# First tile's softmax weights: turned in 32 by 32 blocks by VectorE and put in place by transfers, with the table of the feed-forward blocks laid out anew

## The chip, the cores and the metric

The kernel runs on one core of one Trainium2 chip. The metric is the device time in microseconds (us) of one execution. Five queues matter: PE (TensorE, with PEld for its weight loads), DVE (VectorE), ACT (ScalarE), POOL (GpSimd) and SP (SyncE, which issues transfers and does no arithmetic). Each works through its instructions in the order in which the program issues them; between queues only semaphores wait.

## The reference

Sixteen sequences of 256 tokens with 128 features go through four residual blocks, each applied to a layer-normed copy: a state-space block, a feed-forward block, a power-attention block, and the feed-forward block again.

```python
x = x + ssm(layernorm(x))
x = x + ffn(layernorm(x))
x = x + power_attention(layernorm(x))
x = x + ffn(layernorm(x))
```

The change touches only the feed-forward blocks. Each has two layers, and a layer holds windowed attention and then a gated hidden stage:

```python
qkv = shift_token(x) @ wqkv                # 8 heads of 64
q, k = rotary(l2norm(q) * qs, l2norm(k) * ks)
sim = where(mask, -inf, q @ k.T * 8)       # windows of 64: own window and the one before, 128 keys
x = x + (softmax(sim) @ v) @ wo
h = layernorm(shift_token(x)) * lg + lb
a, g = split(h @ w1 + b1)
x = x + (a * gelu(g)) @ w2 + b2
```

With 256 tokens a sequence has four windows. The kernel takes the first 128 tokens as tile 0 (keys 0 to 127 for all of its queries) and the last 128 as tile 1 (each half of its queries with another 128 keys).

## The kernel before

**Stages.** The program runs the state-space block, feed-forward block 1, the power block and feed-forward block 3, with a little overlap between neighbours. A feed-forward block (`ffn_block`, line 737) handles 32 items, 16 sequences times two layers, in 16 groups of two (n = 2g and 2g + 1).

**The table.** Lines 1111 to 1127 hold one period as a list of words, written out by hand or by a program, in the order of issue. In `we0.1:4` the letters are the step (`stages`, line 1102), the digits its part (tile, half, chunk), `.1` says which of the two sequences of the group, and `:4` how many periods that group lags behind. So one pass through the table works on several groups at different stages. Every engine is wrapped in `Pinned` (line 79), which keeps the written order on each queue, SP among them. Within each engine a step that has to wait holds up all that stands behind it. No step is moved at run time.

**Softmax weights.** For each sequence and tile: `mask` (k, ACT writes the band into a pair of PSUM banks), `scores` (s, PE adds q k), `maxima` (mx, DVE), `less_maximum` (lm, DVE, into SBUF tile `pr`, queries on partitions), `exponentials` (e, ACT), `sums` (su, DVE with a reciprocal), `weights_of` (wo, POOL multiplies). To multiply by the values PE needs keys on partitions: `turn_weights` (wt, line 972) turns one half of the heads, four 128x128 transposes into a PSUM bank, and `turned_weights` (wc, line 980) copies the bank to `prT` on ACT. Then `weigh` (we, line 985, PE), `weighed` (oc, ACT), `mix` (mi, PE) and `mixed` (ma, DVE adds to `u_all`). There is one pair of banks for scores, and six single banks for everything else.

**What SP carries.** `values_out` (vc, line 883) ends for tile 1 with two transfers that make the half-shifted keys' values. `mixed` (ma, line 1013) ends for tile 1 with three transfers that write the shifted tokens into `shifted`; `unit_stats` (Us, line 1029) reads them, tile by tile, with four `bn_stats` of which the last two need the transfers of the group's second sequence. After Us come `unit_factors` (Uf) and `unit_norm` (Un) on POOL, `unit_turn` (Ut) on PE and the gated hidden stage (Ur, Ug, Um, Ud, Ua).

**Memory.** All feed-forward tiles are cut from one SBUF tile, `mem`, by an `Arena` (line 570): an early region from the bottom up and a late one (`FFN_LATE`, lines 732 to 735) up to the top. On the page and in the trace all of them are called `mem`, and nearly every instruction is put down to line 88, the line of `Pinned` that records it.

Of the kernel before, what the change touches and what calls it, by code (L numbers as in the profile page):

```python
# [12 lines left out]
F32 = mybir.dt.float32  # L13
# [7 lines left out]
P = 128  # L21
# [10 lines left out]
WINDOW = 64  # L32
# [13 lines left out]
def kernel(ctx: ExitStack, tc: tile.TileContext, io, out: bass.AP):  # L46
# [555 lines left out]
    class Banks:  # L602
# [11 lines left out]
        def bank(self, q, key, shape, name):  # L614
            b = next((b for b in self.free if b not in self.kept), self.free[0])
            self.free.remove(b)
            self.taken[id(q), key] = b
            q[key] = shaped(self.singles[b][: shape[0], : int(np.prod(shape[1:]))], shape)
            return q[key]

        def give_back(self, q, key):
            self.free.append(self.taken.pop((id(q), key)))
            return q.pop(key)
# [27 lines left out]
    NP = HEADS // 2  # L651
# [77 lines left out]
            layers.append(dict(wq=wq, wo=wo, w1=w1, w2=w2, b1=b1, b2=b2, lg=lg, lb=lb, rope=rope))  # L729
        fw.update(bands=bands, primer=primer, layers=layers)  # L730

    FFN_LATE = [("rn", 32, 2), ("qkT", 2048, 2), ("vx", 1536, 4), ("pr", 1024, 3), ("prT", 1024, 2), ("oT", 512, 2)]
    FFN_LATE += [("mx", 8, 4), ("rl", 8, 4), ("shifted0", 512, 1), ("shifted1", 512, 1), ("hn", 512, 1)]
    FFN_LATE += [("hnT", 512, 1), ("hid", 1536, 1), ("ub", 512, 1)]
    FFN_LATE += [(f"ln_{x}4", 4 * n, 4) for x, n in (("st", 6), ("mv", 2), ("r", 1), ("mr", 1))]

    def ffn_block(k, fw, store, shared):


        mem, ps, pe, dve, act, pool, sp = shared  # L740
        bank, give_back = ps.bank, ps.give_back
        sb = Arena(
            mem,
            [("hT0", 256, 1), ("hT1", 256, 1), ("sq", 512, 2), ("m2", 1024, 2), ("m", 512, 8), ("ss", 32, 2)]
            + [(f"ln_{x}2", 2 * n, 4) for x, n in (("st", 6), ("mv", 2), ("r", 1), ("mr", 1))],
            FFN_LATE, mem.shape[1] - sum(n * c for _, n, c in FFN_LATE),
        )
# [8 lines left out]

        hTs = [sb.tile([P, L], F32, f"f{k}_hT{i}", f"hT{i}") for i in range(2)]
        shifted = [sb.tile([P, GT, D], F32, f"f{k}_shifted{i}", f"shifted{i}") for i in range(2)]
        first = []

        def begin():
# [154 lines left out]
        def mask(n, q, t):  # L916

            psim = q["sim", t] = ps.pair(q, ("sim", t)).rearrange("p r (h k) -> p r h k", h=NP)


            if not first:
                first.append(n)
                for r in range(2):
                    pe.matmul(psim[:, r].rearrange("p h k -> p (h k)"), identb, fw["primer"], start=True, stop=True)
                for h in shifted:
                    pool.memset(h[:1, 0::2, HD:], 0.0)
            act.copy(
                psim.rearrange("p r h k -> p (r h) k"), fw["bands"][t].unsqueeze(1).to_broadcast([P, 2 * NP, P])
            )
# [47 lines left out]
            sb.free(pr, 2)  # L977


        def turned_weights(n, q, t, r):  # L980
            if r == 0:
                q["prT", t] = sb.tile([P, 2, NP, P], F32, name=f"f{k}_prT_{n}_{t}", tag="prT")
            act.copy(q["prT", t][:, r], give_back(q, ("ppt", t, r)))

        def weigh(n, q, t):

            prT, vx = q.pop(("prT", t)), q["vx"]
            po = bank(q, ("po", t), [P, NP, P], f"f{k}_po_{n}_{t}")
            for p in range(NP):
                for w in range(t + 1):  # L990
                    qs = slice(w * WINDOW, (w + 1) * WINDOW) if t else slice(0, P)
                    for r in range(2):
                        pe.matmul(
                            po[r * DH : (r + 1) * DH, p, qs], vx[:, 2 - w if t else 0, 2 * p + r, :],
                            prT[:, r, p, qs], start=True, stop=True,
                        )
            sb.free(prT)
            sb.free(vx, 2)


# [91 lines left out]
        def unit_sum(g, q):  # L1092
# [10 lines left out]
            ns=norm_stats, nf=norm_factors, n=norm, ut=turn_tokens, uc=turned_tokens, p=project, sq=squares,  # L1103
            ro=rotate, ss=square_sums, ra=rotated, v=values, vc=values_out, b=bounded, i=inverses,
            nw=newton, no=normed, t=turn, tc=turned, k=mask, s=scores, mx=maxima, lm=less_maximum,
            e=exponentials, su=sums, wo=weights_of, wt=turn_weights, wc=turned_weights, we=weigh,
            oc=weighed, mi=mix, ma=mixed, Us=unit_stats, Uf=unit_factors, Un=unit_norm, Ut=unit_turn,
            Uc=unit_turned, Ur=unit_rise, Ug=unit_gate, Um=unit_gated, Ub=unit_base, Ud=unit_fall,
            Ua=unit_sum,
        )  # L1110
        period = """
            ns.0:0 Uf:5 p00.0:2 e1.1:4 ma0.0:4 ro01.0:2 t11.0:3 s0.0:3 tc11.0:3 ro11.1:3 oc1.0:4
            v0.0:2 sq00.0:2 su1.1:4 ra11.1:3 Ud0:6 vc0.0:2 Un:5 mx0.0:3 t10.0:3 wt00.1:4 ss00.0:2
            tc10.0:3 wt01.1:4 lm0.0:3 wc00.1:4 Ud1:6 ra01.0:2 wc01.1:4 i.1:3 mi1.0:4 n.0:1 wo1.1:4
            p11.0:2 ma1.0:4 Ua:6 v1.0:2 ro00.0:2 nw.1:3 sq11.0:2 k1.0:3 p10.0:2 ss01.0:2 ra00.0:2
            vc1.0:2 p00.1:2 ro11.0:2 Ut:5 no00.1:3 s1.0:3 Uc:5 no01.1:3 e0.0:3 we0.1:4 mx1.0:3
            ra11.0:2 sq10.0:2 nf.1:1 oc0.1:4 ut.0:1 wt10.1:4 ss10.0:2 wt11.1:4 lm1.0:3 wc10.1:4
            Ur10:5 uc.0:1 wc11.1:4 Ur11:5 ss11.0:2 e1.0:3 ro10.0:2 b.0:2 we1.1:4 no11.1:3 k0.1:3
            su0.0:3 ra10.0:2 t00.1:3 oc1.1:4 v0.1:2 tc00.1:3 su1.0:3 no10.1:3 t01.1:3 vc0.1:2
            p01.1:2 sq00.1:2 wo0.0:3 Ur12:5 tc01.1:3 ss00.1:2 sq01.1:2 ro00.1:2 mi0.1:4 i.0:2 Ug:5  # L1120
            wo1.0:3 s0.1:3 ma0.1:4 ro01.1:2 mi1.1:4 nw.0:2 Ur01:5 ma1.1:4 mx0.1:3 ra00.1:2 p10.1:2
            ss01.1:2 t10.1:3 Ub:5 sq10.1:2 Um1:5 t11.1:3 tc10.1:3 v1.1:2 lm0.1:3 tc11.1:3 no00.0:2
            wt00.0:3 vc1.1:2 wt01.0:3 no01.0:2 ss10.1:2 ns.1:0 wc00.0:3 p01.0:1 ro10.1:2 wc01.0:3
            no11.0:2 Ur00:5 k1.1:3 ra01.1:2 wt11.0:3 Um0:5 e0.1:3 wt10.0:3 Us:4 we0.0:3 n.1:1
            ra10.1:2 wc10.0:3 sq01.0:1 s1.1:3 oc0.0:3 su0.1:3 wc11.0:3 ut.1:1 p11.1:2 mx1.1:3
            wo0.1:3 Ur02:5 uc.1:1 Um2:5 t00.0:2 t01.0:2 no10.0:2 tc00.0:2 lm1.1:3 we1.0:3 sq11.1:2
            tc01.0:2 nf.0:0 mi0.0:3 ss11.1:2 k0.0:2 b.1:2
        """
        parts = []
        for word in period.split():  # L1130
# [3 lines left out]
        for i in range(N // GS + max(lag for *_, lag in parts)):  # L1134
            for j, (step, part, which, lag) in enumerate(parts):
                g = i - lag
                if 0 <= g < N // GS:
                    n = g if which is None else g * GS + int(which)
# [362 lines left out]
    for block, length, ahead in (  # L1501
        (ffn_block(1, fw, False, shared), 39.2, 0.0), (power_block(w, dram, shared), 20.5, 60.0),
        (ffn_block(3, fw, True, shared), 39.2, 20.0),
    ):
        begin, work = block
        start = end - ahead
        line.append((start, begin, ()))
        line += [(start + at * length, step, args) for at, step, args in work]
        end = max(at for at, *_ in line)
# [55 lines left out]
```

## Time and profile before

| what | value |
|---|---|
| median of 3 runs | 2170.4 us (2170.24 to 2171.72) |
| the profiled execution's own time | 2171.14 us |
| its span, first to last instruction | 2169.3 us |
| mean granted TensorE clock | 0.981 |
| PE, DVE, ACT, POOL busy | 94%, 85%, 79%, 88% of the span |
| feed-forward blocks, roughly | 500 to 1140 us and 1510 to 2169 us |

An instruction's record runs from its start to its end; on PE and DVE records of neighbours overlap a little, so that what one more instruction costs is the step from one start to the next. A line of the table of windows gives a stretch of the span, its length, and then for PE, PEld, DVE, ACT and POOL the busy time with the number of instructions in brackets, the granted TensorE clock, the share of the transfer engines and their GB/s. A line of a timeline gives start, length, engine, source line, operation, output and input with shapes, and how many like it follow each other; in brackets at its end stands the idle time before it and who ended it. SPq is SP's own queue of transfer issues.

### The profile page before, as it was taken

What the parts mean: (1) busy time and instruction counts of PE and PEld (TensorE: products, weight loads), DVE (VectorE), ACT (ScalarE), POOL (GpSimd) and SP (SyncE); (2) the same over time, 40 slices, a digit from 0 to 9 for tenths busy, and PEclk for the clock granted to TensorE, in tenths of its full rate; (3) what the DMA queues carried; (4) which work ended last, traced back from release to release, by engine and by line L of the source; (5) the groups of instructions that cost most, each with busy time, mean ns of one, the idle gap of its engine ahead of it and who ended that gap; (6) DMA issues with size and microseconds to landing.
All of it is one profiled execution on the core that took longest, in us unless ns stands there. A gap on an engine that the chain in (4) does not pass through costs nothing.

```text
span 2169.3 us, 44282 instructions
## 1 busy us (share of the span) xinstructions
PE 2028.6 (94%) x16172; PEld 1331.3 (61%) x16174; DVE 1841.5 (85%) x3285; ACT 1706.5 (79%) x2879; POOL 1899.4 (88%) x2183
## 2 busy tenths in 40 slices
PE   5999999877999999999998999998899999999997
PEld 2344444334667777777765777775567777777775
DVE  2999999997989888888856999997988888888873
ACT  4777777746888887887865999997788887878874
POOL 7999999967999888888967999996999988888993
PEclk8999999998999999999997999999999999999998
DMA  4333333321001110111103323230010111101110
GB/s 93 97 83 81 98 80 79 79 52 24 18 22 23 23 23 17 23 23 23 23 11 118 101 98 119 84 114 9 21 23 17 23 23 23 23 16 33 28 28 23
DMA packets 97350, 104.21 MB, mean 48 GB/s; under 512 B 51458, under 2 KB 63596, under 8 KB 97132
## 3 DMA queue, kind: packets, MB, share of 16 engines
q1 hardware_dynamic: 96444, 101.22, 18.4%
q8 instruction: 128, 2.10, 0.4%
q14 instruction: 90, 0.74, 0.1%
q10 hardware_dynamic: 688, 0.15, 0.1%
HBM read 40.28 MB, written 2.36 MB: 20 GB/s over the span
## 4 chain that ended last, share of the span: by engine, by line
PE 54%; POOL 17%; DVE 9%; ACT 9%; issue 7%; DMA 2%; SPq 2%; POOLq 0%; DVEq 0%; ACTq 0%
PE bank L88 44%; POOL bx L88 7%; PE pair L88 7%; POOL mem L88 7%; DVE mem L88 6%; ACT mem L88 5%; DVE hs L88 2%; ACT pair L88 2%; SPq L88 2%; POOL hs L88 1%; PE xe_ps L88 1%; DMA mem<-u_all 1%; DMA bb<-reps 1%; POOL sf L88 1%; PE y_ps L88 1%
## 5 line engine op out<-in xcount | busy, mean ns | idle before, releaser
L88 POOL TENSOR_TENSOR mem<-mem 128x256 f32<-128x256 f32 (+5 forms) x1328 | 1156.7, 901 | 88.4 <-DVE mem L88 66.2
L88 ACT COPY mem<-bank 128x512 f32<-128x512 f32 (+4 forms) x1152 | 590.7, 556 | 147.6 <-PE bank L88 142.0
L88 PEld LDWEIGHTS bank<-ident,mem 128*128 128x128 f32 x3104 | 353.5, 141 | 171.2 <-issue 109.4
L88 PE MATMUL bank<-ident,mem 128*128 128x128 f32 x3104 | 426.0, 277 | 15.1 <-POOL mem L88 10.2
L88 PE MATMUL bank<-wqkv,mem 128*128 128x512 f32 x768 | 385.8, 607 | 1.8 <-ACT mem L88 1.8
L88 DVE TENSOR_REDUCE mem<-mem 128x8 f32<-128x512 f32 (+1 forms) x384 | 325.6, 849 | 9.8 <-ACT mem L88 9.4
L88 DVE TENSOR_TENSOR mem<-bank,rope 128x1024 f32<-128x1024 f32 x256 | 308.8, 1216 | 24.1 <-POOL mem L88 15.8
L88 DVE TENSOR_TENSOR_SCAN hs<-a,bx 128x1024 f32<-128x1024 f32 x128 | 291.4, 2281 | 38.6 <-POOL bx L88 35.5
L88 POOL TENSOR_TENSOR bx<-dx,bb 128x1024 f32<-128x1024 f32 x128 | 298.5, 2357 | 4.0 <-DVE hs L88 3.3
L88 ACT ACTIVATE mem<-mem 128x1024 f32<-128x1024 f32 (+2 forms) x384 | 280.2, 735 | 24.4 <-DVE mem L88 16.3
L88 PE MATMUL pair<-mem 64*64 64x128 f32 (+2 forms) x4096 | 256.7, 296 | 22.0 <-DVE mem L88 13.5
L88 PE MATMUL y_ps<-hs,ident 128*128 128x512 f32 x512 | 242.8, 599 | 11.4 <-DVE hs L88 6.7
L88 PEld LDWEIGHTS pair<-mem 64*64 64x64 f32 (+2 forms) x4096 | 194.9, 160 | 74.2 <-issue 26.2
L88 ACT ACTIVATE a<-delta,neg_a 128x510 f32<-128x510 f32 x256 | 176.0, 689 | 79.1 <-DVE hs L88 73.5
L88 ACT ACTIVATE mem<-bank 128x512 f32<-128x512 f32 (+1 forms) x272 | 160.6, 591 | 62.9 <-PE bank L88 58.6
L88 PE MATMUL bank<-mem 128*64 128x64 f32 (+2 forms) x4608 | 203.3, 255 | 5.3 <-ACT mem L88 2.9
L88 PE MATMUL bank<-mem,w 128*128 128x512 f32 x384 | 193.5, 603 | 3.8 <-ACT mem L88 3.8
L88 PEld LDWEIGHTS bank<-mem 128*64 128x64 f32 (+1 forms) x4608 | 156.8, 128 | 64.3 <-issue 30.1
L88 PEld LDWEIGHTS y_ps<-hs,ident 128*128 128x128 f32 x512 | 95.7, 190 | 154.4 <-issue 125.8
L88 DVE TENSOR_REDUCE mem<-pair 128x8 f32<-128x1024 f32 x128 | 153.2, 1197 | 30.3 <-PE pair L88 29.6
L88 PEld LDWEIGHTS bank<-wqkv,mem 128*128 128x128 f32 x768 | 128.9, 194 | 72.4 <-issue 60.2
L88 DVE TENSOR_TENSOR mem<-pair,mem 128x1024 f32<-128x1024 f32 x128 | 155.5, 1215 | 0.4
(130 smaller groups left out, 2827.0 us busy)
## 6 DMA issues: line engine op xcount, KB each, us to landing
bb<-reps SPq DMA_DIRECT2D x128, 256.0 KB
mem<-pngd SPq DMA_DIRECT2D x64, 512.0 KB
mem<-mem SPq DMA_DIRECT2D x128, 128.0 KB
mem<-u_all SPq DMA_DIRECT2D x64, 64.0 KB
mem<-u_all SPq DMA_DIRECT2D x64, 63.5 KB
x_all<-in_resid_dram SPq DMA_DIRECT2D x8, 256.0 KB
out_dram<-x_all SPq DMA_DIRECT2D x8, 256.0 KB
wqkv<-in_wqkv_dram SPq DMA_DIRECT2D x6, 256.0 KB
```

What stands on the lines that cost most here:

```text
L88: bi = getattr(self.eng, name)(*args, **kw)
```

## The change

In feed-forward blocks tile 0's weights no longer go through PE and ACT. `wt00`, `wt01`, `wc00` and `wc01` leave the table, and two steps enter it. `blocks_turned` (bt) is one DVE instruction over 128x1024 float32 numbers, which turns each 32 by 32 block in its place. `blocks_moved` (bm) issues nine transfers on SP, each of 32 partitions by 1 KB from SBUF to SBUF, one for each block of queries i and block of keys j that the windows allow (1 + 2 + 3 + 3); the rest of the target, `pry0` for even and `pry1` for odd items, is set to zero once for each block of the program, by POOL in the first `mask`. `weigh` for tile 0 reads its moving operand from there, in four runs of 32 numbers in place of one of 128. The late region grows by 4096 numbers for each partition. Tile 1 stays as it was. The table has a new order throughout, with some lags changed (among them Uf and Un from 5 to 4, p00.0 and sq00.0 from 2 to 1, p01.0 and sq01.0 from 1 to 2); its length in the plan that interleaves the blocks stays 39.2.

```diff
+    FFN_LATE = [("rn", 32, 2), ("pry0", 1024, 1), ("pry1", 1024, 1), ("prx", 1024, 2), ("qkT", 2048, 2), ...
...
+        turned_ = [sb.tile([P, NB, 2 * NP, BS], F32, f"f{k}_pry{i}", f"pry{i}") for i in range(2)]
...
+                for y in turned_:
+                    pool.memset(y, 0.0)
...
+        def blocks_turned(n, q):
+            x = q["x"] = sb.tile([P, NB, 2 * NP, BS], F32, name=f"f{k}_prx_{n}", tag="prx")
+            pr = q["pr", 0].rearrange("p r h (b k) -> p b (r h) k", k=BS)
+            dve.transpose(x, pr)
+            sb.free(q["pr", 0])
+
+        def blocks_moved(n, q):
+            x, y = q.pop("x"), turned_[n % 2]
+            q["y"] = y
+            for i in range(NB):
+                for j in range(max(0, i - WINDOW // BS), i + 1):
+                    sp.dma_start(y[j * BS : (j + 1) * BS, i], x[i * BS : (i + 1) * BS, j])
+            sb.free(x)
...
+            if t == 0:
+                prT = q.pop("y").rearrange("k b (r h) q -> k r h b q", r=2)
...
-                            prT[:, r, p, qs], start=True, stop=True,
+                            prT[:, r, p] if t == 0 else prT[:, r, p, qs], start=True, stop=True,
```

The new table, in the words that the prediction follows (the whole has 163 words in place of 167):

```
ns.0:0 we1.0:4 ro01.1:3 bm.1:4 no10.0:3 ut.1:2 ro00.0:2 s0.0:3 ... mx0.0:3 ... vc1.1:3 su1.1:4 ...
lm0.0:3 ... ma0.0:4 ss00.0:2 ... ro01.0:2 ... ma1.0:4 Ua:6 we0.1:4 ss01.0:2 ... ss10.0:2 s1.0:3 ...
su0.0:3 ... mx1.0:3 ... ro10.0:2 ... lm1.0:3 ... ss11.0:2 ... wo0.0:3 ro11.0:2 ... su1.0:3 ...
ro00.1:2 wo1.0:3 mi0.1:4 Ug:5 bt.0:3 s0.1:3 ra11.0:2 ma0.1:4 bm.0:3 mi1.1:4 mx0.1:3 p11.1:2
no11.1:3 ma1.1:4 ss00.1:2 Ur00:5 lm0.1:3 sq11.1:2 p10.1:2 n.0:1 i.0:2 ro11.1:2 nw.0:2 t10.1:3
v0.1:2 tc10.1:3 ra00.1:2 Um0:5 sq10.1:2 Ur02:5 ss11.1:2 e0.1:3 ut.0:1 no00.0:2 Um2:5 t11.1:3
ns.1:0 we0.0:3 su0.1:3 ... ro10.1:2 oc0.0:3 s1.1:3 vc1.0:2 ... Us:4 ... mx1.1:3 ... Uf:4 ...
ss10.1:2 ... Um1:5 ... lm1.1:3 ... ss01.1:2 Un:4 sq00.0:1 bt.1:3 tc01.0:2 mi0.0:3 k0.0:2
```

More of the change, by code (lines that the diff above doesn't have):

```diff
@@ L730, in ffn_weights @@
         fw.update(bands=bands, primer=primer, layers=layers)
-    FFN_LATE = [("rn", 32, 2), ("qkT", 2048, 2), ("vx", 1536, 4), ("pr", 1024, 3), ("prT", 1024, 2), ("oT", 512, 2)]
+    FFN_LATE = [("rn", 32, 2), ("pry0", 1024, 1), ("pry1", 1024, 1), ("prx", 1024, 2), ("qkT", 2048, 2), ("vx", 1536, 4), ("pr", 1024, 3), ("prT", 1024, 2), ("oT", 512, 2)]
     FFN_LATE += [("mx", 8, 4), ("rl", 8, 4), ("shifted0", 512, 1), ("shifted1", 512, 1), ("hn", 512, 1)]
@@ L758, in ffn_block @@
         shifted = [sb.tile([P, GT, D], F32, f"f{k}_shifted{i}", f"shifted{i}") for i in range(2)]
+        BS = 32
+        NB = P // BS
+        turned_ = [sb.tile([P, NB, 2 * NP, BS], F32, f"f{k}_pry{i}", f"pry{i}") for i in range(2)]
         first = []
@@ L985, in weigh @@
         def weigh(n, q, t):
-            prT, vx = q.pop(("prT", t)), q["vx"]
+            vx = q["vx"]
+            if t == 0:
+                prT = q.pop("y").rearrange("k b (r h) q -> k r h b q", r=2)
+            else:
+                prT = q.pop(("prT", t))
             po = bank(q, ("po", t), [P, NP, P], f"f{k}_po_{n}_{t}")
@@ L994, in weigh @@
                             po[r * DH : (r + 1) * DH, p, qs], vx[:, 2 - w if t else 0, 2 * p + r, :],
-                            prT[:, r, p, qs], start=True, stop=True,
+                            prT[:, r, p] if t == 0 else prT[:, r, p, qs], start=True, stop=True,
                         )
-            sb.free(prT)
+            if t == 1:
+                sb.free(prT)
             sb.free(vx, 2)
@@ L1105, in ffn_block @@
             nw=newton, no=normed, t=turn, tc=turned, k=mask, s=scores, mx=maxima, lm=less_maximum,
-            e=exponentials, su=sums, wo=weights_of, wt=turn_weights, wc=turned_weights, we=weigh,
+            e=exponentials, su=sums, wo=weights_of, wt=turn_weights, wc=turned_weights, bt=blocks_turned, bm=blocks_moved, we=weigh,
             oc=weighed, mi=mix, ma=mixed, Us=unit_stats, Uf=unit_factors, Un=unit_norm, Ut=unit_turn,
@@ L1111, in ffn_block @@
         period = """
[L1112 to L1127, printed above, removed]
+            ns.0:0 we1.0:4 ro01.1:3 bm.1:4 no10.0:3 ut.1:2 ro00.0:2 s0.0:3 b.1:3 uc.1:2 no11.0:3
@@ new lines, in ffn_block @@
+            e1.1:4 Ud0:6 mx0.0:3 ra01.1:3 i.1:3 oc1.0:4 vc1.1:3 su1.1:4 t10.0:3 nw.1:3 Ud1:6
+            tc10.0:3 lm0.0:3 wo1.1:4 p01.0:2 nf.0:1 ma0.0:4 ss00.0:2 t11.0:3 sq01.0:2 mi1.0:4
+            no00.1:3 tc11.0:3 ro01.0:2 k1.0:3 Ut:5 p10.0:2 ra00.0:2 ma1.0:4 Ua:6 we0.1:4 ss01.0:2
+            sq10.0:2 no01.1:3 e0.0:3 ss10.0:2 s1.0:3 Uc:5 ra01.0:2 su0.0:3 wt10.1:4 Ub:5 wt11.1:4
+            wc10.1:4 nf.1:1 p11.0:2 mx1.0:3 oc0.1:4 wc11.1:4 t00.1:3 ro10.0:2 Ur11:5 tc00.1:3
+            sq11.0:2 v0.0:2 lm1.0:3 ra10.0:2 t01.1:3 vc0.0:2 ss11.0:2 Ur12:5 tc01.1:3 wo0.0:3
@@ new lines, in ffn_block @@
+            ro11.0:2 e1.0:3 p00.1:2 k0.1:3 we1.1:4 su1.0:3 b.0:2 no10.1:3 sq00.1:2 Ur10:5 oc1.1:4
+            ro00.1:2 wo1.0:3 mi0.1:4 Ug:5 bt.0:3 s0.1:3 ra11.0:2 ma0.1:4 bm.0:3 mi1.1:4 mx0.1:3
+            p11.1:2 no11.1:3 ma1.1:4 ss00.1:2 Ur00:5 lm0.1:3 sq11.1:2 p10.1:2 n.0:1 i.0:2 ro11.1:2
+            nw.0:2 t10.1:3 v0.1:2 tc10.1:3 ra00.1:2 Um0:5 sq10.1:2 Ur02:5 ss11.1:2 e0.1:3 ut.0:1
+            no00.0:2 Um2:5 t11.1:3 ns.1:0 we0.0:3 su0.1:3 tc11.1:3 no01.0:2 k1.1:3 v1.0:2 ra11.1:2
+            ro10.1:2 oc0.0:3 s1.1:3 vc1.0:2 vc0.1:2 Us:4 wo0.1:3 Ur01:5 uc.0:1 n.1:1 wt10.0:3
@@ L1128, in ffn_block @@
+            mx1.1:3 wt11.0:3 Uf:4 wc10.0:3 p01.1:2 ss10.1:2 wc11.0:3 p00.0:1 Um1:5 sq01.1:2 ra10.1:2
+            lm1.1:3 t00.0:2 t01.0:2 tc00.0:2 v1.1:2 ss01.1:2 Un:4 sq00.0:1 bt.1:3 tc01.0:2 mi0.0:3
+            k0.0:2
         """
```

## The prediction

> **What bounds the kernel now.** I read the shares and slices of the page first, then engine sums by stretch, then timelines of PE, DVE and SP inside one period, and last SP's rows.
>
> ```profile
> PE 2028.6 (94%) x16172; PEld 1331.3 (61%) x16174; DVE 1841.5 (85%) x3285; ACT 1706.5 (79%) x2879; POOL 1899.4 (88%) x2183
> PE   5999999877999999999998999998899999999997
> ...
> 545.00:584.00 39.00, 36.66 (x376) 26.69 (x376) 36.46 (x62) 31.52 (x60) 37.68 (x54) 1.00 0.10 22
> 623.74:662.82 39.08, 39.08 (x357) 27.99 (x357) 35.15 (x57) 32.96 (x60) 37.14 (x56) 1.00 0.10 22
> 858.24:897.32 39.08, 39.08 (x357) 27.99 (x357) 33.59 (x49) 31.60 (x56) 33.67 (x44) 1.00 0.10 22
> ```
>
> The table of windows shows it: from 623.7 to about 1107 us (12.4 periods) PE is busy for all of each 39.08 us period, and block 3 repeats this. PE is the only bound there; DVE idles 5.5 us of a late period. In the first periods, while norm statistics (ns, nf, n) still run, DVE has 35.15 and POOL 37.14; two such periods, 623.7 to about 702, are PE-bound, and the two before them are bound by POOL (37.7 of 39.0).
>
> **PE and ACT: removed.** The timeline of PE, one period:
>
> ```profile
> 882.38 1.04 PE L88 MATMUL bank<-ident,mem 128*128 128x128 f32 x8
> 883.25 1.02 PE L88 MATMUL bank<-wqkv,mem 128*128 128x512 f32 x2
> ```
>
> Eight transposes take 0.87 us from start to start, 0.108 each; a period loses 16: 1.73 us. PE's new sum is 39.08 - 1.73 = 37.35. ACT loses four 0.59 us copies and bounds nothing. `weigh` keeps its matmuls; for its split moving operand I take the same price (nearest: 633 ns for the convolution's split 128x512 operand against 595 to 607, so 0 to 6% of 2 x 1.03 us, under 0.15 us).
>
> The Trainium skill ("VectorE: DVE Perf Modes", Rules for kernel authors) advises TensorE for a 128x128 transpose where the result may land in PSUM, and VectorE only for 32x32 blocks within a bank: a rule against this change. Its table (The three transpose paths) gives TensorE 390 ns for bf16; by that, as an estimate, the removed part would be 16 x 0.39 = 6.2 us of a period; by the row it is 1.73, and the row decides.
>
> **DVE: added.** No block transpose is in the trace. Bounds for 128x1024: 0.60 (step after a 128x512 reduce, in case two numbers go per cycle) and 2.26 us (two passes of the 1.13 step); I take 1.2, the recorded length of other 128x1024 float32 instructions (1193 to 1216 ns). DVE's sum becomes 33.59 + 2 x 1.2 = 36.0 late, 37.5 early: still at or under PE.
>
> **SP: added, and in the way.** Nine transfers for each item stand in one run. The rows of SP, and the timeline of SP and DVE round Us:
>
> ```profile
> 9.77 1.82 SPq L166 DMA_DIRECT2D wd2T<-in_wd2T_dram  x4
> 786.47 4.64 SPq L88 DMA_DIRECT2D mem<-u_all  x3
> 791.22 1.20 SPq L88 DMA_DIRECT2D mem<-mem  x2
> ...
> L88 SPq DMA_DIRECT2D mem<-mem x128: 461/549/1512, 503.7 to 2089.6; - x128
> L88 SPq DMA_DIRECT2D mem<-pngd x64: 319/320/433, 1143.2 to 1449.8; - x64
> ...
> 2084.15 4.65 SPq L88 DMA_DIRECT2D mem<-u_all  x3
> 2091.20 0.29 DVE L88 BATCH_NORM_STATS2 mem<-mem 128x6 f32<-128x128 f32 x1 [0.37 <-DMA mem<-u_all]
> ```
>
> One issue, d, costs between 0.37 (320 ns plus a 0.05 gap) and 0.65 (0.60 each in the x2 row plus a gap); I take 0.50, between the nearest in shape (wd2T, 16 rows of 1 KB, 0.455 each) and the nearest in kind (SBUF to SBUF, 0.60). A run is 9 x 0.50 = 4.5 us. SP's sum is harmless (2 x (4.65 + 1.20 + 4.5) = 20.7 of 37), its order is not: in the new table bm.0 stands directly ahead of ma1.1, so the three transfers of `mixed` queue behind it. From their first issue to the third `bn_stats` of Us (the one that reads them) is 7.05 us in the rows above.
>
> [...]
>
> **The loop.** bt.0 on DVE 1.2, bm.0 on SP 4.5, the transfers of ma1.1 7.1, then DVE in written order until bt.0 of the next period. That work, by steps from start to start in the late period: the last two statistics 0.8; mx 3 x 1.13; su 3 x 1.36; lm 3 x 1.13; ro 6 x 1.13; ss 6 x 0.60; bt.1 1.2; Um1 0.67; Ua 0.60; two ma 0.4: 24.9 us. Sum 1.2 + 4.5 + 7.1 + 24.9 = 37.7. This exceeds PE's 37.35, though DVE's own sum is 36.0: DVE stands idle for some 2 us before Us. Early, ns.0 adds 0.8: 38.5. POOL's way round (Us, Uf, Un ... wo0.0, bt.0) has about 21.4 us in place of 24.9 late, 24.2 in place of 25.7 early, and does not decide. Meshing: before, nothing is lost; in the power stage (1250 to 1450) the fullest engine, ACT, shows 49.3 to 49.6 of 50; I add 0.2. Late 37.9, early 38.7.
>
> y's own transfers are nearly hidden: 1.2 + 4.5 + 2.4 (7.05 - 4.65, from the last issue to use) = 8.1 us from bt.0; PE has s0.1, mi1.1, five 0.87 projections, two turns and ut.0, 7.5 us, before we0.0. The 0.6 left over fits in PE's slack, 37.9 - 37.35. If PE were late, weigh, v1.0 and s1.1 behind it would be late too.
>
> **Once per block.** At its end, where nothing covers it, tile 0 takes 8.1 us in place of two turns and two copies (2 x (0.43 + 0.59) = 2.0); tile 1 follows tile 0 by mask, scores, mx and lm (1.03 + 1.05 + 1.13 + 1.13 = 4.3) and hides part of that, while we0.1 stands ahead of wt10.1 on PE: 3 us (0 to 6). Two memsets of 128x1024 on POOL at 952 ns (row of the power block's), in a stretch where POOL is full: 1.0 (0 to 1.9). The larger late region now overlaps the power block's `vx`, whose zeroing stands half a period behind the last we0 in the plan: nothing.
>
> **Sum.** A block: late 10.4 x (39.08 - 37.9) = 12.3; two early x (39.08 - 38.7) = 0.8; the two before them 0, POOL's load being the same; less 3 and 1: 9.1. Two blocks 18.2. From the profiled execution's 2171.1: 2152.9; the median lies 0.7 lower: **2152 us**.
>
> **Rivals.**
> - *PE stays the bound* (d at 0.37 to 0.42; for: transfers of the power block at 320 ns; against: all SBUF-to-SBUF ones at 0.46 and more). Loop 36.5 to 37.0, period 37.35 + 0.2: 10.4 x 1.53 + 2 x 1.0 - 2.5 = 15.4, two blocks 31: 2140. With nothing lost at all, 2 x 12.4 x 1.73 = 43: 2127.
> - *Slower: SP's queue.* Same loop at d = 0.65: 39.05 + 0.2 late, 40.05 early. Block: -1.8, -1.9, the two before -1, end -4, memset -1.9: -10.6; 2192. It decides from d = 0.58, where 9.1 is used up (each 0.1 of d is 0.9 us in 12.4 periods). For: the x2 row; against: that row follows the long u_all transfers directly.
> - *Slower: block transpose at 2.26.* Both bt lie in the loop: 37.9 + 2.1 = 40.0, early 40.8; -9.6 - 3.4 - 2 - 5: -20 a block; 2210. Decides from about 1.6 us.
> - *Nothing to measure:* d near 0.56 to 0.60, gains and once-per-block costs cancel: 2166 to 2175.
>
> That the change does something else than it says is out: the built order holds 64 block transposes, 576 small transfers and 512 fewer turns.
>
> **How the numbers follow.** Under 0.2% (4.3 us) a difference can't be told from none. Forecast (d 0.43 to 0.56, 2144 to 2166) 0.35, PE stays the bound 0.25, nothing to measure 0.11, SP slower 0.20, transpose slower 0.09. Faster 0.60, same 0.11, slower 0.29. Range: 2130 (between 2140 and 2127) to 2194, which takes in SP's rival and leaves out the slow transpose.
>
> **What would show it.** Period in PE's chain: 37.4 PE-bound, 37.7 to 38 loop, 39 and over SP. DVE's third `bn_stats` of Us idle on "DMA mem<-u_all" by about 2 us each period; SP's run x9 of 4.1 to 5.9 us with u_all's x3 right behind; StreamTranspose near 1.2 us; PE idle about 0.5 us a period, on ACT's mask or on the new transfers. Wrong if DVE never waits at Us (the loop is not there), if PE waits longest at we0 (y's way is the bound), or if the new order loses a microsecond elsewhere.

## The result and the profile after

The changed kernel takes 2233.5 us (median of four runs, 2231.2 to 2237.1) beside 2171.0 us for the kernel before on the same chip: 1.029 times as long, 95% interval 1.0276 to 1.0301. The forecast was 2152 us, a gain of 18 us, with a range up to 2194; the change costs 62 us instead.

The page of the changed kernel, its shares of busy time and PE's forty slices:

```profile
PE 2004.3 (90%) x15662; PEld 1282.4 (58%) x15662; DVE 1909.2 (86%) x3349; ACT 1662.9 (75%) x2751; POOL 1903.7 (85%) x2187
...
PE   6999999867899999999978999997789999999986
```

PE is busy for 24 us less than before (2028.6 to 2004.3), and for 90% of a longer span in place of 94%: in the slices of the feed-forward blocks the nines at both ends of a block give way to eights and a seven.

Three windows of 39 us, about a period, with the columns of the windows shown before the forecast; the first is at the start of a feed-forward block, the second early in it, the third late:

```profile
556.00:595.00 39.00, 33.54 (x338) 23.06 (x336) 34.64 (x56) 27.34 (x51) 33.39 (x49) 0.96 0.15 36
638.50:677.74 39.24, 36.77 (x331) 24.87 (x330) 35.82 (x58) 31.49 (x54) 35.27 (x50) 1.00 0.15 34
863.81:903.05 39.24, 38.37 (x345) 26.21 (x348) 35.62 (x52) 30.11 (x51) 33.68 (x45) 1.00 0.15 37
```

From the first transfer of one `ma1.1` to that of the next, a late period is 39.24 us (860.33 to 899.57), against 39.08 before, although PE has sixteen turns less to do in it; early periods are up to 40.5 us (661.52 to 701.99). In the late window PE is busy for 38.37 us, DVE for 35.62, POOL for 33.68: all have room, so the period is set by waits between them. The timelines of DVE and SP over that period show the ring that the forecast had described:

```profile
867.51 0.29 DVE L88 BATCH_NORM_STATS2 mem<-mem 128x6 f32<-128x128 f32 x1 [2.80 <-DMA mem<-u_all]
...
892.54 1.24 DVE L88 STREAM_TRANSPOSE mem<-mem 128x1024 f32<-128x1024 f32 x1
...
906.74 0.29 DVE L88 BATCH_NORM_STATS2 mem<-mem 128x6 f32<-128x128 f32 x1 [2.79 <-DMA mem<-u_all]
```

```profile
893.84 5.63 SPq L88 DMA_DIRECT2D mem<-mem  x9
899.57 4.62 SPq L88 DMA_DIRECT2D mem<-u_all  x3
```

Followed round: from the third `bn_stats` of Us to the block transposition, DVE's own written order, 892.54 - 867.51 = 25.03 us; to SP's first issue 1.30; nine issues up to the first transfer of `mixed` 5.73; from there to the third `bn_stats` of the next group 906.74 - 899.57 = 7.17. The sum is 39.23 us, which is the period, as it must be for any way from one event to its next. What makes this way the one that binds is that nothing on it has slack: DVE's timeline shows no idle time from 867.51 to 892.54, SP begins 0.06 us after the transposition's end, and the three transfers follow the nine at 0.10 us. Each turn of the ring ends in 2.8 us in which DVE waits for the transfers. Over the execution that wait is 100.1 us in 32 places; before it was 14.3 us in 9:

```profile
DVE mem L88 <- DMA mem<-u_all: 100.1, 32, 6.5
```

How much longer each stretch got can be read from when `ma1.1` of each group issues its first transfer (the row of 127x2x64 on SP). The spans, 2169.3 and 2228.8 us, differ by 59.5:

| stretch | first feed-forward block | second |
|---|---|---|
| up to the first `ma1.1` of the block (for the second, from the last one of the first) | +11.0 | +10.3 |
| the 13 periods between | +8.7 | +9.0 |
| the last two periods | +13.2 | +8.6 |

The end of the program gives 1.3 us back. So the loop, which the forecast expected to gain 13.1 us a block, lost about 9, and starts and ends of the blocks, which it had at 4 us a block, cost 24 and 19.

### The profile page after: what moved, and what is told of

Read it like the earlier page. It is cut to its first block, busy times and chain, and to the rows that moved or that the text cites. A ratio compares the mean times of both kernels' runs of the same rounds, so it can differ in the third digit from the quotient of the medians.

```text
span 2228.8 us, 43918 instructions
## 1 busy us (share of the span) xinstructions
PE 2004.3 (90%) x15662; PEld 1282.4 (58%) x15662; DVE 1909.2 (86%) x3349; ACT 1662.9 (75%) x2751; POOL 1903.7 (85%) x2187
## 5 line engine op out<-in xcount | busy, mean ns | idle before, releaser
L88 POOL TENSOR_TENSOR mem<-mem 128x256 f32<-128x256 f32 (+4 forms) x1328 | 1158.2, 899 | 87.5 <-DVE mem L88 40.3
L88 ACT COPY mem<-bank 128x512 f32<-128x512 f32 (+3 forms) x1024 | 524.2, 551 | 227.4 <-PE bank L88 219.5
L88 PE MATMUL bank<-wqkv,mem 128*128 128x512 f32 x768 | 398.8, 611 | 6.6 <-DVE mem L88 4.8
L88 PEld LDWEIGHTS bank<-ident,mem 128*128 128x128 f32 x2592 | 298.0, 142 | 165.6 <-issue 107.3
L88 PE MATMUL bank<-ident,mem 128*128 128x128 f32 x2592 | 371.5, 279 | 22.2 <-POOL mem L88 17.1
L88 PE MATMUL bank<-mem 128*64 128x64 f32 (+2 forms) x4608 | 209.3, 258 | 52.9 <-DMA mem<-mem 22.1
L88 PEld LDWEIGHTS bank<-mem 128*64 128x64 f32 (+1 forms) x4608 | 163.0, 130 | 128.2 <-DVE mem L88 36.8
L88 PE MATMUL bank<-mem,w 128*128 128x512 f32 x384 | 201.9, 613 | 2.5 <-ACT mem L88 2.5
L88 POOL TENSOR_SCALAR mem<-mem 128x32 f32<-128x32 f32 (+2 forms) x256 | 62.0, 242 | 134.8 <-DVE mem L88 116.4
```

The source lines that it names most:

```text
L88: bi = getattr(self.eng, name)(*args, **kw)
```

## The experiments

The theory after the result: nine issues in one run on SP, at 0.626 us each, make the ring longer than PE's period, and the same run is laid bare where a block fills and drains. The rivals: the new order of the table costs this by itself; or the transfers, not their issue, are what is slow. Each time is set against the kernel before on the same chip, where that took 2170.8 to 2171.8 us.

### Four transfers in place of nine

```diff
-                for j in range(max(0, i - WINDOW // BS), i + 1):
+                for j in range(i, i + 1):
                     sp.dma_start(y[j * BS : (j + 1) * BS, i], x[i * BS : (i + 1) * BS, j])
```

> Only the four transfers on the diagonal (i = j) of the nine are issued; the five others are left out, so part of tile 0's weights is missing from the output. Theory A (SP's run of nine issues, 5.63 us, holds back the three transfers of mixed in the middle of a block and the first tile's weights at both of its ends): the run falls to 2.5 us, the loop from about 39.2 to about 36.1, so that PE bounds the late periods at 37.4 to 37.7; 13 periods of a block win some 1.7 us each, its two ends 3 us each: about 2 x 28 us less than the changed kernel's 2233, so 2170 to 2185. Theory B (the new order of the table is worse by itself, whatever the transfers cost): the period stays above 39 and the time above 2220.

Measured: 2141.0 us, 0.986 of before (0.9843 to 0.9876), and 92 us less than the changed kernel. SP's timeline, one period:

```profile
872.05 2.46 SPq L88 DMA_DIRECT2D mem<-mem  x4
874.61 4.57 SPq L88 DMA_DIRECT2D mem<-u_all  x3
```

The run of issues is 3.2 us shorter, the middle periods 37.58 us, PE busy for all of them, and DVE has no wait for u_all left there. That is PE's sum of the forecast, 37.35, and 0.2. The gain is larger than the 48 to 63 us that theory A had: by the starts of `ma1.1`'s transfers the 26 periods gave 51 us (44 expected) and the starts and ends of the blocks 37 (12 expected). The same edit takes five transfers away as well as five issues, so it does not part the two.

### The new order alone, with PE's turns

The new table with `wt00 wc00 wt01 wc01` in the place of each `bm`, no `bt`, and `weigh` reading PE's result:

```diff
-            ... ro01.1:3 bm.1:4 no10.0:3 ...
+            ... ro01.1:3 wt00.1:4 wc00.1:4 wt01.1:4 wc01.1:4 no10.0:3 ...
-            ... bt.0:3 s0.1:3 ra11.0:2 ma0.1:4 bm.0:3 mi1.1:4 ...
+            ... s0.1:3 ra11.0:2 ma0.1:4 wt00.0:3 wc00.0:3 wt01.0:3 wc01.0:3 mi1.1:4 ...
```

> The new order of the table alone: wt00, wc00, wt01, wc01 stand where bm stood, bt and the zeroing are gone, tile 0 is turned by PE as before. Theory A: without the run on SP the order does no harm, PE bounds the periods at 39.1 again and the ends are as before: 2165 to 2180. Theory B: the slow starts and ends of the blocks (about +11 and +9 to +13 us each) come from the order and stay: 2205 or more. If only a part of them is the order's, the time lies between, and its distance from 2171 is that part.

Measured: 2191.6 us, 1.0092 of before (1.0077 to 1.0107): between the two expectations. The middle periods are 39.74 us, 0.66 longer than before with the same work on PE. PE's waits come to 1.4 us over six of them, 0.24 each; the rest is longer steps of the same instructions, of the projections above all (24 matmuls of 128x512: 10.70 us in place of 10.42), and why is open. It is a price of this order with PE's turns in it; without the turns the same order runs at 37.58 us a period (the run above), 0.2 above PE's forecast sum, so it is at most a small part of what the changed kernel lost.

### Nine transfers behind those of `ma1.1`

```diff
-            ... ma0.1:4 bm.0:3 mi1.1:4 ... ma1.1:4 ss00.1:2 ...
+            ... ma0.1:4 mi1.1:4 ... ma1.1:4 bm.0:3 ss00.1:2 ...
```

With it `we0.0` goes behind v1.1:2, `oc0.0` behind tc01.0:2, and `mi0.0` behind Ud0 of the next period (lag 4).

> All transfers stay, but in the table bm.0 moves behind ma1.1, and we0.0, oc0.0 and mi0.0 move to the end of the period, where y has landed. Theory A: the statistics of Us no longer wait for bm.0; the late period falls from 39.2 to 37.4 to 37.9, the early one from 40.5 to about 39; starts and ends stay as they are or grow by 1 to 3 us: 2190 to 2210. If the wait at Us is not what sets the period (another loop as long lies beside it), the period stays at 39 and the time at 2225 to 2240.

Measured: 2175.0 us, 1.0017 of before (1.0007 to 1.0026), 58 us less than the changed kernel with every transfer still there and still on SP. That is more than theory A expected, which had the starts unchanged: they got 10 and 8 us shorter, while the middle periods, 38.42 us, stay above its 37.4 to 37.9. PE idles for 1.04 us in each of them:

```profile
922.35 1.10 PE L88 MATMUL pair<-mem 64*64 64x128 f32 x32 [0.73 <-ACT pair L88]
...
931.47 1.16 PE L88 MATMUL pair<-mem 64*128 64x128 f32 x16 [0.31 <-ACT pair L88]
```

The ring is gone and PE waits only for ACT's mask. The ends stay long: the last two periods take 33.9 and 29.5 us (before 31.3 and 24.4), because `we0.1` still stands behind nine issues:

```profile
1115.61 3.68 PE L88 MATMUL bank<-mem 128*64 128x128 f32 x48 [5.34 <-DVE mem L88]
```

The view names DVE, whose transposition had long ended. SP begins the run that `we0.1` needs at 1107.95; nine issues of 0.626 us end at 1113.6, and PE starts 2.0 us later.

### Issues or transfers: half the bytes, and a second queue

Half the bytes (heads 4 to 7 are left out of the transfers):

```diff
-                    sp.dma_start(y[j * BS : (j + 1) * BS, i], x[i * BS : (i + 1) * BS, j])
+                    sp.dma_start(y[j * BS : (j + 1) * BS, i, :NP], x[i * BS : (i + 1) * BS, j, :NP])
```

> The nine transfers stay in place and in number, but each moves only four of the eight heads (32 partitions x 512 B in place of 1 KB); the weights of the other four heads stay zero in tile 0, which is left out of the computation. It measures the term that the forecast had at 0.50 us and the trace at 0.626 us. Theory E (the price is per issue): SP's run of nine stays 5.4 to 5.7 us and the time 2225 to 2240 us. Rival F (the price follows the bytes or the DMA engines' work): the run shrinks to 2.8 to 4.5 us, the middle periods to 37.5 to 38.3 us and the time to 2140 to 2190 us.

Measured: 2228.3 us in one run, SP's run unchanged:

```profile
890.43 5.63 SPq L88 DMA_DIRECT2D mem<-mem  x9
896.16 4.61 SPq L88 DMA_DIRECT2D mem<-u_all  x3
```

The price is per issue, 0.626 us, at 512 B a partition as at 1 KB.

The four diagonal blocks issued from ScalarE's queue:

```diff
-                    sp.dma_start(y[j * BS : (j + 1) * BS, i], x[i * BS : (i + 1) * BS, j])
+                    eng = act if i == j else sp
+                    eng.dma_start(y[j * BS : (j + 1) * BS, i], x[i * BS : (i + 1) * BS, j])
```

> All nine transfers stay where the changed kernel has them, but the four of the diagonal blocks are issued from ScalarE's queue and only five from SP's; nothing is left out. Theory A (SP's run of issues is the cost, the transfers themselves are not): SP's run becomes 5 x 0.626 = 3.1 us, the loop 24.9 + 1.24 + 3.1 + 7.05 = 36.3 us, under PE's 37.4 us, so the middle periods take 37.5 to 37.8 us as they did with four transfers alone and the time is 2138 to 2155 us, if ScalarE (30 us of 37.6 busy) takes four issues without delay. Rival B (the nine transfers get in each other's way on the DMA engines, whoever issues them): middle periods stay above 39 us and the time above 2200 us. Rival C (an issue holds ScalarE as long as it holds SP, 2.5 us twice per period, in front of the evictions that PE waits for): 38 to 39 us per period, 2160 to 2200 us.

Measured: 2245.9 us, 1.034 of before (1.0323 to 1.0358): worse than the changed kernel, and worse than rival C priced it. ACT's timeline has the reason:

```profile
859.09 3.22 ACTq L88 DMA_DIRECT2D mem<-mem  x3
862.40 0.60 ACT L88 ACTIVATE mem<-bank 128x512 f32<-128x512 f32 x1 [3.04 <-PE bank L88]
...
875.58 2.45 ACTq L88 DMA_DIRECT2D mem<-mem  x4
878.07 0.75 ACT L88 COPY mem<-bank 64x256 f32<-64x256 f32 x2 [2.53 <-DMA mem<-mem]
```

ACT computes nothing while it issues: it idles 3.04 and 2.53 us beside issues of 3.22 and 2.45 us. DVE's wait for u_all falls from 100.1 to 15.0 us over the execution (14.3 before), so SP's part went as theory A had it, but the evictions behind the issues stand still, and then PE, POOL and DVE wait in turn; from the third period on the periods take 39.3 to 43.6 us. The issue costs as much on this queue as on SP's (2.45 / 4 = 0.61 us), and while both queues issue, SP's five take 3.54 us (0.71 each) in place of 3.10. The time alone would have fitted rival B, transfers slowed by each other. The idle ACT says C, and against B stand the run with nine transfers behind those of `ma1.1`, 58 us faster than the changed kernel, and the run with half the bytes, which changed nothing.

### The diagonal without transfers

A diagonal block stays on its partitions, so ScalarE can copy it, with five transfers left on SP:

```diff
-                for j in range(max(0, i - WINDOW // BS), i + 1):
+                for j in range(max(0, i - WINDOW // BS), i):
                     sp.dma_start(y[j * BS : (j + 1) * BS, i], x[i * BS : (i + 1) * BS, j])
+            for i in range(NB):
+                act.copy(y[i * BS : (i + 1) * BS, i], x[i * BS : (i + 1) * BS, i])
```

> The four diagonal blocks do not change partitions, so ScalarE copies them (four copies of 32 x 256) and SP issues only the other five; the order is the changed kernel's, nothing is left out. Theory A: SP's run 3.1 us, ScalarE's copies about 4 x 0.25 us twice per period beside 7 us of idle time, middle periods 37.5 to 37.8 us, 2138 to 2155 us, equal to the run with a split queue within 0.5%. Rival C (ScalarE's written order makes the copies wait for the transposition in front of evictions): 38 to 39 us per period, 2160 to 2200 us.

Measured: 2161.4 us, 0.9953 of before (0.9938 to 0.9968). The whole computation is done, in 72 us less than the changed kernel. SP's run is 3.10 us and the middle periods 37.88 us; DVE's wait for u_all is gone from them. The time lies in rival C's range and the period just above theory A's. Only the way of the four diagonal blocks differs from the run with two queues, and it makes 85 us: copies of 1.65 us on ACT (the expectation had four of 0.25) in place of issues of 2.4 to 3.8. The longest wait in the middle periods, POOL's for ACT (1.4 us at most in the run of four transfers), sits behind the copies, which stand directly behind ACT's table load:

```profile
877.15 1.65 ACT L88 COPY mem<-mem 32x256 f32<-32x256 f32 x4
```

```profile
880.07 0.58 POOL L88 TENSOR_TENSOR mem<-mem 128x32 f32<-128x32 f32 x2 [3.17 <-ACT mem L88]
```

PE is busy throughout all the same, so the view alone does not show that this wait makes the 20 us above the run of four; the copies' place is tried below.

### Starts and ends against the loop

The same relief for groups 0, 1, 2, 14 and 15 of each block alone:

```diff
+            relieved = not 3 <= n // GS < N // GS - 2
...
+                    if i == j and relieved:
+                        act.copy(y[j * BS : (j + 1) * BS, i], x[i * BS : (i + 1) * BS, j])
+                    else:
                         sp.dma_start(y[j * BS : (j + 1) * BS, i], x[i * BS : (i + 1) * BS, j])
```

> The relief (diagonal blocks by ScalarE, five transfers on SP) for the sequences of groups 0, 1, 2, 14 and 15 of each block alone; the groups between keep nine transfers; nothing is left out. It parts what the forecast did not cost, the starts and ends of the blocks, from the loop that it did. From the starts of the transfers in the two traces the relieved stretches are worth some 37 us of the 72 us between 2233 and 2161. Theory A (the prices of starts and ends are SP's run as well, and stand beside the loop's): 2190 to 2205 us, middle periods 39.2 us. Rival H (the starts only wait for what the loop would make them wait for anyway, so that a relieved start is paid back in the loop): 2215 to 2235 us.

Measured: 2196.5 us, 1.0118 of before (1.0103 to 1.0134). Of the 72 us that the whole relief is worth, 37 come from the first three and the last two groups of the blocks; the other 35, by subtraction, are the loop's between, whose periods stay at 39.2 us. What a relieved start gains is not paid back in the loop.

### The order of the kernel before, with the block steps

```diff
-            ... ma1.1:4 mx0.1:3 ... wt00.0:3 ... wt01.0:3 ... wc00.0:3 ... wc01.0:3 ... we0.0:3 ... we1.0:3 ...
+            ... bt.0:3 ma1.1:4 bm.0:3 mx0.1:3 ... we0.0:3 oc0.0:3 we1.0:3 ...
-            ns.0:0 Uf:5 ... wt00.1:4 ... wt01.1:4 ... wc00.1:4 ... wc01.1:4 ...
+            ns.0:0 bm.1:4 Uf:5 ... b.1:2 bt.1:3
```

(The first pair of lines is from the middle of the table, the second from its beginning and end; `oc0.0` stands directly behind `we0.0`.)

> All nine transfers on SP, but in the order of the kernel before: its table, with the eight turn and copy steps of tile 0 taken out, the two block steps put in around ma1.1 (transposition ahead of it, transfers behind it) and at the period's end and beginning, and we0.0 and oc0.0 moved behind the turns of the next scores; nothing is left out. Theory A (the order of the new table costs 20 us by itself, as it did with PE's turns, and SP's run lies behind ma1.1 here): 2150 to 2168 us, middle periods 37.6 to 38.3 us. Rival D (the order matters only through the place of the transfers): the same as with the new table and the transfers behind ma1.1, 2170 to 2180 us, middle periods 38.4 us.

Measured: 2264.1 us, 1.0428 of before (1.039 to 1.0466): both expectations missed. The periods are 39.8 to 43.7 us, and PE waits for the transfers at the weighing:

```profile
922.83 3.33 PE L88 MATMUL bank<-mem 128*64 128x128 f32 x48 [2.90 <-DMA mem<-mem]
```

SP's issues of `mixed` come first and the nine behind them, and the some 4 us of PE's steps that now stand ahead of `we0.0` (s1.1, ut.1, two steps of 0.87, two turns) don't cover that. This says that this insertion into the old order was bad, and nothing of whether that order could carry the change better.

### Where the copies stand

The copies as a step of their own, `bd`, and the five transfers where they were:

```diff
-            ... e0.1:3 ut.0:1 ...                    ... sq01.0:2 mi1.0:4 ...
+            ... e0.1:3 bd.0:3 ut.0:1 ...             ... sq01.0:2 bd.1:4 mi1.0:4 ...
```

> As the run with the diagonal blocks copied by ScalarE (2161 us, middle periods 37.88 us, POOL waiting 3.2 us per period on ScalarE behind the copies), but the copies are a step of their own, 3 to 8 us later in ScalarE's order; nothing is left out. Theory A (what is left above the run of four, 20 us, is ScalarE held at the copies): middle periods 37.6 us, the starts of the blocks as with four transfers, 2141 to 2152 us. Rival G (the fifth transfer on SP, or the copies' own 1.65 us, makes it): 2157 to 2165 us.

Measured: 2187.9 us, 1.0082 of before (1.0065 to 1.0099), with middle periods of 39.2 us. The expectation of a gain failed, and so did rival G's: the place makes 26 us in the other direction. POOL's wait shrank, but PE now waits at `we0.0` for the copies:

```profile
889.75 1.09 PE L88 MATMUL bank<-mem 128*64 128x128 f32 x16 [1.26 <-ACT mem L88]
```

Between the two places, with `we0.0` one projection later:

```diff
-            ... i.0:2 ro11.1:2 ... we0.0:3 su0.1:3 ... v1.0:2 ra11.1:2 ...        ... uc.1:2 no11.0:3 ...
+            ... i.0:2 bd.0:3 ro11.1:2 ... su0.1:3 ... v1.0:2 we0.0:3 ra11.1:2 ... ... uc.1:2 bd.1:4 no11.0:3 ...
```

> The diagonal blocks copied by ScalarE as a step of its own, but only some 2 us later than in the run of 2161 us (behind the bound of the inverses that POOL waits for, and for the other sequence behind the copy of its turned tokens), with we0.0 one projection later; nothing is left out. Theory J (the copies' place in ScalarE's order is worth several us per period in either direction: too early holds POOL by 3.2 us, too late holds PE by 1.5 us): between the two places POOL waits less than 2 us and PE not at all, middle periods 37.5 to 37.8 us, 2145 to 2158 us. Rival G (the copies and the fifth transfer cost what they cost wherever they stand): 2159 to 2190 us.

Measured: 2150.1 us, 0.9906 of before (0.9891 to 0.9921): faster than both kernels, with nothing left out. The window of one middle period, 37.42 us, and POOL's longest wait in it:

```profile
863.81:901.23 37.42, 37.42 (x341) 26.12 (x340) 35.59 (x50) 32.75 (x60) 33.75 (x46) 1.00 0.14 32
```

```profile
876.23 0.58 POOL L88 TENSOR_TENSOR mem<-mem 128x32 f32<-128x32 f32 x2 [0.96 <-ACT mem L88]
```

PE is busy without a break and the period is its sum of the forecast, 37.35, to 0.07 us. The copies and `we0.0` were moved together, so their shares of the 11 us are not parted.

One more step, the five transfers behind those of `ma1.1`, the rest as in the last run:

```diff
-            ... ma0.1:4 bm.0:3 mi1.1:4 ... ma1.1:4 ss00.1:2 ...
+            ... ma0.1:4 mi1.1:4 ... ma1.1:4 bm.0:3 ss00.1:2 ...
```

> As the run with the copies 2 us later, and the five transfers of the first sequence stand behind ma1.1's instead of ahead of them; nothing is left out. If SP's run still limits anything with five transfers, this frees another 3.1 us of the loop: middle periods 37.4 to 37.6 us and 2140 to 2155 us, below the run without it. If the loop is PE's by then, the middle periods stay and the ends of the blocks decide, within 10 us of the run without it; if the transfers land too late for we0.0, PE waits on them and the time is 2165 to 2185 us.

Measured: 2288.1 us, 1.0542 of before (1.0525 to 1.056), the slowest of all and far outside what was expected. The five transfers now land after `we0.0` wants them:

```profile
1005.29 1.09 PE L88 MATMUL bank<-mem 128*64 128x128 f32 x16 [3.39 <-DVE mem L88]
```

```profile
996.08 4.54 SPq L88 DMA_DIRECT2D mem<-u_all  x3
1000.73 19.93 SPq L88 DMA_DIRECT2D mem<-mem  x14
```

(The second row holds waits of SP as well as issues.) The five begin to issue at 1000.73, in place of ahead of the u_all issues, and at 0.62 us each are issued by about 1003.8; PE stands at `we0.0` until 1005.29, though DVE's transposition, which the view names, came long before. The middle periods get 3.5 us longer (40.9), which is about PE's wait; the first six of a block take 42.3 to 44.3. The step that brought nine transfers 58 us costs five transfers 138, because `we0.0` stands one projection later than in the changed kernel here, and ten steps of PE, some 7 us, later there.

## Why the prediction was wrong

**PE's part: right.** Sixteen turns at 0.108 us were to leave 37.35 us. Where nothing else limits, the periods are 37.42 us with five transfers (and `we0.0` later) and 37.58 with four. `weigh` kept its price with the split operand.

**The block transposition: right.** Taken at 1.2 us between 0.60 and 2.26. The row of the late stretch (count, then sum in us and mean in ns):

```profile
L88 DVE STREAM_TRANSPOSE mem<-mem 128x1024 f32<-128x1024 f32 x11 | 13.6, 1235 | 0.0
```

It falls in with the 1.19 to 1.22 us of the other instructions that the forecast went by, so the rival of the slow transposition is out.

**The loop: right mechanism, and the failing step is d, the price of one issue.** The ring through bt.0, bm.0, ma1.1's transfers and Us is what the trace shows, and moving bm.0 out of it, or shortening it, ends DVE's wait. Its terms measured against the forecast: 25.0 to 24.9, 1.3 to 1.2, 7.2 to 7.1, and 5.7 to 4.5. The forecast took d as 0.50, between the nearest row in shape and the nearest in kind; the run shows 0.626. The row of the right kind, SBUF to SBUF at 0.60, was in the profile, and averaging it with a load from DRAM was the mistake: the trace has other prices for other kinds (319 ns from the power block's DRAM copy), but it showed none below 0.46 us for this kind. Half the bytes left the issue at the same price, so bytes were the wrong thing to go by; what in the kind makes the price was not tried. With d at 0.626 the forecast's own sum gives 38.8 + 0.2 = 39.0 late; the period is 39.2, and the first four of a block take 39.7 to 40.7. By that sum d alone turns the gain of 13.1 us a block into a loss of about 1 (10.4 x 0.05 less 2 x 0.75, an estimate). Of the 8.7 and 9.0 us lost, another 3.1 and 3.2 lie in the first of the 13 periods, 39.8 and 40.0 us after 36.7 before, which the forecast had at no loss; the rest is mostly in the other early ones. It is the forecast's rival "SP's queue", which had 0.20 of the chance, decided "from d = 0.58". (The forecast had DVE's early sum "at or under PE"; 35.15 + 2.4 = 37.55 is over PE's 37.35, which decided nothing beside the longer ring.)

**Once per block: the other failing step, four us taken for some twenty.** The forecast had "3 us (0 to 6)" for the end and 1.0 for the memsets, and counted the start at nothing else. The two ends cost 13.2 and 8.6, the starts 11.0 and 10.3. Of the 78 us between the forecast's 2152.9 and the profiled execution's 2231.2 the loop makes 44 and starts and ends 34. Even the rival's 2192 us was 41 us short, and starts and ends are 31 of these: 43 in the table, of which it had 2 x (4 + 1.9). The end of the first block, on SP and PE:

```profile
1146.66 5.61 SPq L88 DMA_DIRECT2D mem<-mem  x9
1152.38 17.01 SPq L88 DMA_DIRECT2D mem<-u_all  x6
```

```profile
1135.32 1.64 PE L88 MATMUL bank<-mem 128*64 128x128 f32 x16 [2.81 <-DMA mem<-mem]
...
1154.02 1.98 PE L88 MATMUL bank<-mem 128*64 128x128 f32 x16 [5.35 <-DMA mem<-u_all]
```

`we0.0` waits 2.81 us and `we0.1` 5.35 us for their runs; the view names u_all for the second, but `we0.1` reads only the nine, issued by 1152.27. The forecast priced one such wait per block, but in the last two periods four items go through the run, with less and less beside them. Where a block fills, the first `we0.0` waits as well, again under DVE's name:

```profile
545.58 1.98 PE L88 MATMUL bank<-mem 128*64 128x128 f32 x16 [2.08 <-DVE mem L88]
```

A second thing slows PE there, its clock. The same 16 matmuls take 1.64 to 1.98 us in these rows, in place of 1.09 us in a late period. The granted clock (the last number but two) is 0.50 round the rows of 1.98 and 1.00 in the late period:

```profile
545.30:548.50 3.20, 2.92 (x18) 2.11 (x18) 1.55 (x3) 0.59 (x1) 3.20 (x5) 0.50 0.17 41
1152.90:1159.50 6.60, 5.49 (x27) 4.16 (x28) 0.00 (x0) 1.57 (x3) 3.13 (x6) 0.50 0.13 26
861.90:863.10 1.20, 1.11 (x17) 0.97 (x17) 1.17 (x3) 0.95 (x2) 1.20 (x2) 1.00 0.08 17
```

Such stretches are there in the kernel before as well, but fewer: the mean clock is 0.974 in place of 0.981. As an estimate from these means and the spans, (1 - 0.974) x 2228.8 less (1 - 0.981) x 2169.3, they cost up to 17 us of PE's time, which no term of the forecast had. In the run of 2150.1 us, whose mean clock is 0.981, nothing of that is left. How much of the 43 us is waiting and how much the clock was not parted.

With four transfers the ends cost nothing more than before, and 3.0 and 2.8 us of the starts remain. How much of the starts is the zeroing of the two targets (two memsets of 942 ns, as forecast) was not tried apart, nor why 1.7 of the first 11.0 us are lost already ahead of the block's first step.

**y "nearly hidden": true in the middle only.** The 0.6 us left over are there, in PE's slack:

```profile
861.99 1.09 PE L88 MATMUL bank<-mem 128*64 128x128 f32 x16 [0.68 <-DMA mem<-mem]
```

**The new order "elsewhere"**: named as what could make the forecast wrong, and not the cause. It costs 20 us with PE's turns in it; without them its periods come to within 0.2 us of PE's forecast sum.

The gain that the forecast counted on was there to be had: with five issues in place of nine the same idea gives 2150.1 us.

The Trainium skill ("DMA: Bandwidth & Descriptors", Issuing engines are not separate DMA queues) says that issuing from several engines only saves the sequencer's time to initiate a transfer, which it calls usually small beside the transfer. The run with two queues agrees with the first half: with four issues taken off SP, DVE's wait for u_all fell to 15.0 us. The second half did not hold here: 0.61 to 0.63 us an issue stand beside some 2.0 us from the last issue to PE's start, nine in a row set the period, and moving four of them to a computing engine cost 12 us more than leaving them on SP.

## What to carry to other kernels

Price a new transfer by its issue: take the row of the same kind (here SBUF to SBUF on the same queue), not of the same size, multiply it by the length of the run, and walk the ring in which the run stands, since queue time between two engines that both have room can still set the period. Count such a chain at each fill and drain of a pipeline, once for every item in flight and not once for a block. Before small transfers are added, look for those that change no partition (an idle engine may copy them), and place the copies where the next reader needs them: a few us earlier or later made 11 to 38 us here (in the best place with `we0.0` one projection later as well). Read the granted clock where a pipeline fills and drains, too: it was 0.50 in places here.

## What the runs showed of the hardware

- An issue of 32 partitions by 1 KB from SBUF to SBUF holds SP for 0.61 to 0.63 us in runs of four to nine, at 512 B a partition as at 1 KB (5.63 us for nine both times).
- ACT's queue pays 0.61 us for the same issue, and ACT computes nothing meanwhile (2.53 us idle beside four issues of 2.45). When SP and ACT issue at the same time, SP's run of five goes from 3.10 to 3.54 us.
- A 32x32 block transposition of 128x1024 float32 numbers on DVE takes 1235 ns, close to the reductions and two-input instructions of that size in this kernel (1197 to 1216 ns); a copy of 32x256 on ACT takes 0.41 us.
- TensorE's granted clock was 0.50 for some us at a time where the blocks fill and drain, and 16 matmuls of 128x128 float32 took 1.98 us there, in place of 1.09 us at 1.00.
